# Two layers on a graph of 3327 nodes on one core: products with v spread one, none, two over three rounds, side pieces in other rounds, counts of adj in a row of their own

## The chip, the core and the metric

The kernel runs on one core of one Trainium2 chip. The metric is the device time of one execution in microseconds (us); the time before is the median of three executions. All views come from one profiled execution of the program.

Engines are named as in the profile: PE multiplies matrices (PEld is its loading of weights), ACT applies functions such as the exponential, DVE and POOL work element by element, SP issues nearly all DMAs. Each engine has its own queue, and the engines wait for each other through semaphores.

## The reference, cut to what matters

N = 3327 nodes with 128 features, adj a 0/1 matrix of N x N with about 0.24% ones and a full diagonal.

```python
# layer 0
H = X @ W.T + b;  s = H @ a_s;  r = H @ a_r
e = leaky_relu(A * s + A * r.T, 0.2)
att = softmax(where(A > 0, e, NEG), axis=1)
x = layernorm(x + att @ H)
# layer 1, n = 3327, d = 128, h = 8
q = (x @ Wq.T).reshape(d, n, h)      # k and v likewise
a = einsum('dnh,dmh->dnm', q, k) * d ** -0.5
a = softmax(a + adj + adj, axis=2)
out = einsum('dnm,dmh->dnh', a, v).reshape(n, h * d) @ Wo.T
x = layernorm(x + out)
```

Because of the reshape, layer 1 has 128 independent attentions ("d") of 3327 queries and 3327 keys, each with only 8 numbers per key. Their 128 x 3327 x 3327 exponentials are nearly the whole work. adj is added twice; the kernel takes the exponential with a scale of 2, so it adds adj once to half-scaled scores, or multiplies the exponential by a factor made of adj (e squared where adj is 1, else 1).

## The kernel before, in words

**Main work.** The 128 attentions go in 32 groups of four; each group has seven blocks of 476 queries (the last 472), so there are 224 blocks. In a block the 26 tiles of 128 keys are taken in 26 rounds. Two plans alternate: even blocks take eight threes of key tiles and then a pair (24, 25); odd blocks take tile 25, then eight threes, then tile 24. A round works on two halves of tiles; a half is two of the four attentions, 128 x 952 numbers.

A three is a *stretch* of three rounds, here called A, B, C. Its first tile, x, is handled on ACT and POOL: scores on PE (L152), an exponential straight from the scores (L1172), and a multiplication by the factor on POOL (L1173). The other two are added on DVE: scores plus adj (L1175), and in a later round one exponential over both halves, 128 x 1904 (L991).

| round | scores and what follows |
|---|---|
| A | half 1 of x; half 0 of the first added tile |
| B | half 0 of x; half 1 of the first added tile |
| C | both halves of the second added tile |

Score banks: one for x, two for added tiles, so x's scores in B wait until ACT has read those of A. Round 1 of an even block issues its two pairs of scores in reverse order.

**Products with v** (L956, `products`): one key tile against v for four attentions, eight matmuls summed into a single bank `av` over the block. `multiply` puts the round's tile into the list `waiting` and multiplies the tile four rounds back (LAG = 4), so each round has one product, behind the round's scores and side piece on PE. The tile is one that ACT or POOL finished in earlier rounds. After a block's last product DVE copies `av` out (L966), and the next block's first product waits for that copy. In odd blocks the copy is put between the two adds of round 3 (`between`).

**Side pieces.** Layer 0 for the later row tiles, the projections to q, k and v, and the results of layer 1 are cut in pieces and slipped into the rounds. Two rows hold them in order. `main` has, for each of 25 row tiles, 26 products (26 key tiles with weighed adj, L241), the normalization and twelve projections, and later the results; `aside` has the weighing and masking of adj on POOL (L308, L317; nine pieces of each for a row tile, three key tiles a piece) and the counts of adj on DVE (L326; 18 pieces) and, in between, the loads of adj. Kinds are p (PE), d (DVE), l (DVE, a round later), m (POOL), x (issues DMAs); `n` entries wait for a mark and `t` entries set one. `lane` says in which rounds one piece of a kind may go: before, p, d and m in the rounds for which `reading` holds (round 1 of every three, counted from the first three, with exceptions at the ends of a block), so in B of a stretch.

`aside` is a strict order: weighing and masking of one chunk of adj (six pieces), then the six counts of a chunk, then the load of a later chunk.

**The first seven blocks** also make the factors of adj on POOL (L793), stretch by stretch, and store them; later blocks load them.

The nested functions that the diff touches stand in the order-building part of the kernel; nothing in it is chosen at run time, so each engine's order is fixed when the program is built.

Of the kernel before, what the change touches and what calls it, by code (L numbers as in the profile page):

```python
# [17 lines left out]
P = 128  # L18
# [29 lines left out]
def kernel(  # L48
# [29 lines left out]
    H = wqT.shape[1]  # L78
# [71 lines left out]
    def special():  # L150
# [9 lines left out]
        with ExitStack() as sx, tc.manual_schedule(engines=ALL):  # L160
# [9 lines left out]
            CH = [(i, min(i + CW, NT)) for i in range(0, NT, CW)]  # L170
# [96 lines left out]
            def layer0(t, side=True, trow=None, bank=bank, held=None):  # L267
# [5 lines left out]
                s = {"a": {}, "w": {}}  # L273
                q0 = t * len(CH)
# [55 lines left out]
                def product(i):  # L330
                    if i == 0:
                        s["p"] = bank()
                    (by_columns if side else whole)(
                        s["p"][:, : D + 1],
                        s["w"][i // CW][: kr[i], i % CW, :],
                        hsb[: kr[i], i, :],
                        r,
                        start=(i == 0),
                        stop=(i == NT - 1),
                    )  # L340
# [124 lines left out]
                for n, (i0, i1) in enumerate(CH):  # L465

                    aside.append(("n", ("P", q0 + n - 2, 0)))
                    for c0 in range(i0, i1, 3):
                        c1 = min(c0 + 3, i1)
                        aside.append(("m", lambda n=n, c0=c0, c1=c1: weigh(n, c0, c1)))  # L470
                        aside.append(("m", lambda n=n, c0=c0, c1=c1: mask(n, c0, c1)))
                    aside.append(("t", ("W", q0 + n)))
                    c = [("d", lambda n=n, h=h, k=k: count(n, h, k)) for h in range(3) for k in range(2)]
                    counts.append(c)
                    main.append(("n", ("W", q0 + n, 3)))
                    if i1 == NT:
                        main.append(("m", biased))
                    main += [("p", lambda i=i: product(i)) for i in range(i0, i1)] + [("t", ("P", q0 + n))]
                    aside.append(counts[-1])
                return loads, main + chain + [("t", ("rows", t))], aside  # L480

            def result(t):
# [116 lines left out]
                units += [("p", lambda: turn(0, 2, 0)), ("p", lambda: turn(2, 4, 2))]  # L599
                units += [("d", lambda: divided(0, 2, 0)), ("d", lambda: divided(2, 4, 2))]  # L600
                units += [("p", lambda: turn(4, 5, 0)), ("d", lambda: divided(4, 5, 0))]
                units += [("p", lambda h=h: project(h)) for h in range(H)]
                root = rsqrt(s, lambda: s["st"][:r, 7:8], r)
                units += [("d", finish), ("d", together(variance, *root[:3]))]
                return units + [("d", together(*root[c : c + 3])) for c in (3, 6, 9)] + [("d", scale)]
# [368 lines left out]

            waiting = []

            def multiply(s, i):
                waiting.append((s, i))
                while len(waiting) > LAG:
                    products(*waiting.pop(0))  # L980

# [20 lines left out]

            def reading(n, odd):

                n -= odd
                if n % 3 == 1 and 4 <= n < NR - 2:  # L1010
                    return True
                return n in ((NR - 2,) if odd else (0, NR - 1))

            def lane(kind, n, odd):

                if kind == "l":
                    return int(reading(n - 1, odd) if n else True)
                return int(reading(n, odd) or kind == "p" and n - odd == 3)

            made = [layer0(t) for t in range(1, NT)]  # L1020
            first_loads = made[0][0]
            main = []
            aside = []
            for n, (_, m, a) in enumerate(made):

                later = []
                for u in a:
                    if u[0] == "r":

                        at = max((k for k, v in enumerate(aside) if v[0] == "n"), default=0)  # L1030
                        aside.insert(at, ("x", u[1]))
                    elif isinstance(u, list):
                        ahead = made[n + 1][0][sum(isinstance(v, list) for v in later)] if n + 1 < len(made) else None
                        later.append(u)
                        if n:
                            aside += u + [ahead] * (ahead is not None)
                    else:
                        aside.append(u)
                if n == 0:

                    for k, u in enumerate(later):
                        aside += u + [made[1][0][k]] * (len(made) > 1)
                main.append(m)
            main.append([("n", ("counts", 0, 0))] + judge())
            aside.append(("t", ("counts", 0)))
            results = [((needs[t] + 1) * total + LAG + 6, result(t)) for t in range(NT - 1)]
            end = result(NT - 1)
            marks = {("P", q): 0 for q in range(len(CH))}
            side = {"main": [], "aside": aside, "since": {"main": 0, "aside": 0}, "read": -2}

            def head(row, now, force=False):

                while True:
                    if not side[row]:
                        if row == "aside":
                            return None
                        ahead = ("rows", reads[min(max(now, 0) // total + 2, NG - 1)]) in marks
                        if results and results[0][0] <= now and (ahead or not main):
                            side[row] = results.pop(0)[1]
                        elif main:  # L1060
                            side[row] = main.pop(0)
                        else:
                            return None
                    kind, f = side[row][0]
                    if kind == "t":
                        marks[f] = now
                    elif kind == "w":
                        if not force and now - side["since"][row] < f:
                            return None
                    elif kind == "n":  # L1070
                        if f[:2] not in marks or not force and now - marks[f[:2]] < f[2]:
                            return None
                    else:
                        return kind
                    side[row].pop(0)
# [4 lines left out]

            def work_tensor(now, n, odd):

                for _ in range(lane("p", n, odd) if side["read"] != now - 1 else 0):
                    if head("main", now) != "p":
                        break
                    run("main", now)

            def work(now, n, odd):
                room, low, pool = lane("d", n, odd), lane("l", n, odd), lane("m", n, odd)
                for row in ("main", "aside"):  # L1090
                    while True:
                        kind = head(row, now)
                        if kind == "x":
                            pass
                        elif kind == "d" and room:
                            room -= 1
                            if row == "main":
                                side["read"] = now
                        elif kind == "l" and low:
                            low -= 1  # L1100
                            side["read"] = now
                        elif kind == "m" and pool:
                            pool -= 1
                        else:
                            break
                        run(row, now)

            def finish_to(mark, now):
                while mark not in marks:
                    row = "main" if head("main", -1 if now is None else now, True) else "aside"  # L1110
                    if head(row, -1 if now is None else now, True) is None:
                        break
                    run(row, -1)
                    tick(True)
# [13 lines left out]
            for g in range(NG):  # L1128
                k4, v4, _ = group
                for b in range(NBLK):  # L1130
# [5 lines left out]
                    for n, rnd in enumerate(rounds):  # L1136
# [16 lines left out]
                        for j in range(HG):  # L1153
                            if n == NR // 2 + j * (NR > 12) and (b + 1 < NBLK or g + 1 < NG):
                                queries[1](j)
                        sc = {}
                        for i, h, z in reversed(rnd) if n == 1 and not odd else rnd:
                            sc[i, h] = (pe if z is None else pd).tile([P, 2, 512], F32, name="scb")
                            for t in range(2):
                                pair_scores(sc[i, h][: kr[i], t, :w], s.k4, s.q4, i, kr[i], 2 * h + t, w)  # L1160
                        work_tensor(g * total + at, n, odd)
                        between = odd and n == LAG - 1
                        for (i, h, at_) in rnd:
                            if between and h == 1:
                                multiply(s, order[n])
                            r, z = kr[i], sc[i, h]
                            if i not in s.e:
                                s.e[i] = sp.tile([P, HG, WB], F32, name="e4")
# [13 lines left out]
                        if n + 1 in starts or n + 1 == NR:  # L1182
                            del adjs[m]
                            make_factor(m + 1)
                        if not between:
                            multiply(s, order[n])
                        work(g * total + at, n, odd)
            exp_late(NG * total + 2)
            finish_to(None, NG * total + LAG + 6)
# [384 lines left out]
```

## Time and profile before

| what | value |
|---|---|
| time, median of 3 | 10050.16 us (10049.41 to 10050.97) |
| profiled execution, its own time | 10052.42 us |
| its span, first to last instruction | 10050.6 us |
| mean granted PE clock | 0.995 |
| exponentials from scores, L1172 | 3920, mean 1000 ns |
| late exponentials, L991 | 3920, mean 1810 ns |
| POOL's multiplies, L1173 | 3920, mean 2236 ns |
| DVE's adds, L1175 | 7728, mean 1142 ns |
| products, L956 | 46592 matmuls (8 a tile), mean 573 ns |

How to read it: spans of instructions that follow each other on ACT or POOL overlap a little, so the mean of one is longer than the distance from its start to the next one's start. Matmuls of four row or column parts run side by side, so PE's time for a product is the distance from its start to the start of what follows. Busy shares are means over the whole span; where an engine is late is seen in the timeline.

### The profile page before, as it was taken

What the parts mean: (1) busy time and instruction counts of PE and PEld (TensorE: products, weight loads), DVE (VectorE), ACT (ScalarE), POOL (GpSimd) and SP (SyncE); (2) the same over time, 40 slices, a digit from 0 to 9 for tenths busy, and PEclk for the clock granted to TensorE, in tenths of its full rate; (3) what the DMA queues carried; (4) which work ended last, traced back from release to release, by engine and by line L of the source; (5) the groups of instructions that cost most, each with busy time, mean ns of one, the idle gap of its engine ahead of it and who ended that gap; (6) DMA issues with size and microseconds to landing.
All of it is one profiled execution on the core that took longest, in us unless ns stands there. A gap on an engine that the chain in (4) does not pass through costs nothing.

```text
span 10050.6 us, 207550 instructions
## 1 busy us (share of the span) xinstructions
PE 9477.4 (94%) x79523; PEld 3013.9 (30%) x79523; DVE 9188.5 (91%) x10554; ACT 9897.6 (98%) x7904; POOL 9177.2 (91%) x4954
## 2 busy tenths in 40 slices
PE   7999999999999999999999999999999999999998
PEld 2233333333233233323333333333333233222222
DVE  7899999999999999999999999999999999888888
ACT  7999999999999999999999999999999999999998
POOL 7999999999999999999999999999999999888887
PEclk9999999999999999999999999999999999999999
DMA  6765656665665656565566656566665565555554
GB/s 194 209 179 179 179 168 183 178 176 168 181 173 171 183 167 189 168 184 170 169 179 187 176 172 179 176 170 178 181 179 175 171 175 168 169 158 166 164 164 132
DMA packets 1399414, 1755.28 MB, mean 175 GB/s; under 512 B 349360, under 2 KB 1386890, under 8 KB 1394312
## 3 DMA queue, kind: packets, MB, share of 16 engines
q1 hardware_dynamic: 1388061, 1739.30, 59.7%
q8 instruction: 626, 10.26, 0.4%
q10 hardware_dynamic: 10347, 2.61, 0.1%
q14 instruction: 380, 3.11, 0.1%
HBM read 1637.49 MB, written 103.93 MB: 173 GB/s over the span
## 4 chain that ended last, share of the span: by engine, by line
ACT 41%; PE 21%; POOL 16%; issue 13%; DVE 7%; DMA 2%; SPq 1%; POOLq 0%; ACTq 0%; DVEq 0%
ACT e L991 29%; POOL e L1173 15%; ACT e L1172 11%; PE av L956 11%; PE scb L152 9%; DVE e L1175 5%; PE bank L241 1%; DVE o L966 1%; DMA q4b<-qT 1%; DMA at<-in_adjT_dram 1%; POOL w L308 0%; SPq L733 0%; POOL w L317 0%; DMA k4b<-kT 0%; POOL at L793 0%
## 5 line engine op out<-in xcount | busy, mean ns | idle before, releaser
L1173 POOL TENSOR_TENSOR e<-e,at 128x952 f32<-128x952 f32 (+1 forms) x3920 | 8715.9, 2236 | 788.6 <-ACT e L1172 735.1
L1175 DVE TENSOR_TENSOR e<-scb,at 128x952 f32<-128x952 f32 (+1 forms) x7728 | 8499.4, 1142 | 769.7 <-PE scb L152 650.1
L991 ACT ACTIVATE e<-e 128x1904 f32<-128x1904 f32 (+3 forms) x3920 | 7095.9, 1810 | 26.4 <-DVE e L1175 11.1
L956 PE MATMUL av<-e,v4b 128*32 128x476 f32 (+1 forms) x46592 | 5843.8, 573 | 99.0 <-DVE o L966 68.0
L152 PE MATMUL scb<-q4b,k4b 32*128 32x476 f32 (+1 forms) x23296 | 3882.4, 486 | 440.8 <-ACT e L1172 361.9
L1172 ACT ACTIVATE e<-scb 128x952 f32<-128x952 f32 (+1 forms) x3920 | 3921.1, 1000 | 74.9 <-PE scb L152 36.7
L152 PEld LDWEIGHTS scb<-q4b,k4b 32*128 32x128 f32 (+1 forms) x23296 | 1779.3, 189 | 5459.2 <-ACT e L1172 3161.5
L956 PEld LDWEIGHTS av<-e,v4b 128*32 128x32 f32 (+1 forms) x46592 | 1014.1, 109 | 1239.9 <-issue 933.4
L241 PE MATMUL bank<-hsb,w 128*32 128x129 f32 (+1 forms) x5200 | 278.6, 286 | 0.0
L326 DVE TENSOR_SCALAR_CACHE_REDUCE dump<-a 128x384 bf16<-128x384 f32 (+2 forms) x468 | 247.3, 528 | 0.6
L308 POOL TENSOR_SCALAR w<-trow,er 128x129 f32<-128x129 f32 x650 | 231.6, 376 | 1.3
L317 POOL TENSOR_TENSOR w<-w,a 128x384 f32<-128x384 f32 (+3 forms) x225 | 207.9, 924 | 0.1
L966 DVE COPY o<-av 128x476 f32<-128x476 f32 (+1 forms) x224 | 145.2, 648 | 31.3 <-PE av L956 30.4
L241 PEld LDWEIGHTS bank<-hsb,w 128*32 128x32 f32 (+1 forms) x5200 | 102.9, 108 | 148.2 <-issue 148.2
L241 PE MATMUL bank<-wo,ot 128*32 128x128 f32 x1600 | 85.2, 285 | 0.0
L402 DVE TENSOR_SCALAR hi<-bank 128x256 fp32r<-128x256 f32 (+1 forms) x200 | 83.0, 415 | 0.0
L409 DVE SCALAR_TENSOR_TENSOR lo<-bank,hi 128x256 fp32r<-128x256 f32 (+1 forms) x200 | 83.0, 415 | 0.0
L241 PE MATMUL bank<-wk,x1T 128*32 128x256 f32 x800 | 63.9, 391 | 0.0
L241 PE MATMUL bank<-wq,x1T 128*32 128x256 f32 x800 | 63.9, 391 | 0.0
L241 PE MATMUL bank<-wv,x1T 128*32 128x256 f32 x800 | 63.9, 391 | 0.0
L502 PE MATMUL bank<-ident,o 128*128 128x128 f32 x225 | 52.0, 304 | 0.0
L290 POOL MEMSET a<- 128x128 f32 (+1 forms) x25 | 5.2, 208 | 44.4 <-DVE dump L326 44.4
(123 smaller groups left out, 647.3 us busy)
## 6 DMA issues: line engine op xcount, KB each, us to landing
at<-in_adjT_dram SPq DMA_DIRECT2D x1536, 476.0 KB
at<-ftd SPq DMA_DIRECT2D x1674, 238.0 KB
at<-in_adjT_dram SPq DMA_DIRECT2D x256, 472.0 KB
at<-ftd SPq DMA_DIRECT2D x279, 236.0 KB
k4b<-kT SPq DMA_DIRECT2D x128, 415.9 KB
q4b<-qT SPq DMA_DIRECT2D x1528, 29.8 KB
at<-in_adjT_dram SPq DMA_DIRECT2D x192, 208.2 KB
at<-in_adjT_dram SPq DMA_DIRECT2D x150, 238.0 KB
```

What stands on the lines that cost most here:

```text
L152: nc.tensor.matmul(dst, k4[32 * j : 32 * j + H4, first_key(i) : first_key(i) + 2 * r - 1 : 2], q4[32 * j : 32 * j + H4, :nb], start=True, ...
L241: nc.tensor.matmul(dst[c0:c1], w[:, c0:c1], mov, **kw)
L308: nc.gpsimd.tensor_scalar(w, s["t"][:, :, :T3], -LOWEST, e, op0=ALU.min, op1=ALU.max)
L317: nc.gpsimd.tensor_tensor(w, w, s["a"][n][:, c0 - i0 : c1 - i0, :r], op=ALU.mult)
L326: nc.vector.tensor_scalar(z, a, float(k), None, op0=ALU.is_equal, op1=ALU.add, accum_out=even[:, t, at : at + 1])
L402: nc.vector.tensor_scalar(hi[:r, o : o + QW], s["b"][:r, :QW], scale, None, op0=ALU.mult)
L956: nc.tensor.matmul(s.av[32 * j : 32 * j + 32, : s.w], s.v4[:r, j, i * H1 : i * H1 + 32], e[:r, j, : s.w], start=(s.left == NT - 1), stop=( ...
L966: nc.vector.tensor_copy(o4[:, :w], s.av[:, :w])
L991: nc.scalar.activation(e, e, AF.Exp, scale=2.0)
L1172: nc.scalar.activation(eh, z[:r, :, :w], AF.Exp, scale=2.0)
L1173: nc.gpsimd.tensor_tensor(eh, eh, ah, op=ALU.mult)
L1175: nc.vector.tensor_tensor(eh, z[:r, :, :w], ah, op=ALU.add)
```

## The change

The products: B (`place` 1) has none, A (`place` 0) one, and C (`place` 2) two, the first of them between its two pairs of scores. `between` goes, so in odd blocks the copy of `av` comes behind both adds. The side pieces: one p, d or q in A, q also in B, m in B, l in C (q is the new name for the layer-0 products and the results' projections, so these may come twice in a stretch). The counts leave `aside` for a third row, `counts`, together with the loads of adj that follow them; marks L tell `aside` that a chunk's load has been issued, and the loads wait with marks W until the chunk before has been weighed and masked. The numbers of all pieces are as before.

```diff
-                        between = odd and n == LAG - 1
-                        for (i, h, at_) in rnd:
-                            if between and h == 1:
-                                multiply(s, order[n])
+                        for i, h, at_ in rnd:
...
+                        place = (n - odd) % 3
                         for i, h, z in reversed(rnd) if n == 1 and not odd else rnd:
+                            if place == 2 and h == 1:
+                                multiply(1)
                             sc[i, h] = (pe if z is None else pd).tile([P, 2, 512], F32, name="scb")
...
-                        if not between:
-                            multiply(s, order[n])
+                        waiting.append((s, order[n]))
+                        multiply(int(place != 1))
...
-            def multiply(s, i):
-                waiting.append((s, i))
-                while len(waiting) > LAG:
-                    products(*waiting.pop(0))
+            def multiply(k):
+                for _ in range(k):
+                    if len(waiting) > LAG:
+                        products(*waiting.pop(0))
...
-            def reading(n, odd):
+            def lane(kind, n, odd):
                 n -= odd
-                if n % 3 == 1 and 4 <= n < NR - 2:
-                    return True
-                return n in ((NR - 2,) if odd else (0, NR - 1))
-
-            def lane(kind, n, odd):
                 if kind == "l":
-                    return int(reading(n - 1, odd) if n else True)
-                return int(reading(n, odd) or kind == "p" and n - odd == 3)
+                    return int(n % 3 == 2)
+                if kind == "q" and n % 3 == 1:
+                    return 1
+                if kind == "m":
+                    return int(n % 3 == 1)
+                if n % 3 != 0:
+                    return 0
+                return int(kind in "pq" or n > 3 or n == 0 and odd)
...
+                    aside.append(("n", ("L", q0 + n, 0)))
...
-                    main += [("p", lambda i=i: product(i)) for i in range(i0, i1)] + [("t", ("P", q0 + n))]
+                    main += [("q", lambda i=i: product(i)) for i in range(i0, i1)] + [("t", ("P", q0 + n))]
...
-                units += [("p", lambda h=h: project(h)) for h in range(H)]
+                units += [("q", lambda h=h: project(h)) for h in range(H)]
...
                     elif isinstance(u, list):
-                        ahead = made[n + 1][0][sum(isinstance(v, list) for v in later)] if n + 1 < len(made) else None
-                        later.append(u)
-                        if n:
-                            aside += u + [ahead] * (ahead is not None)
+                        counts += u
+                        if n + 1 < len(made):
+                            counts += [("n", ("W", (n + 1) * len(CH) + k, 0)), made[n + 1][0][k], ("t", ("L", (n + 2) * len(CH) + k))]
+                        k += 1
...
-                for _ in range(lane("p", n, odd) if side["read"] != now - 1 else 0):
-                    if head("main", now) != "p":
-                        break
+                kind = head("main", now)
+                if kind in ("p", "q") and lane(kind, n, odd) and side["read"] != now - 1:
                     run("main", now)
...
-                for row in ("main", "aside"):
+                for row in ("main", "aside", "counts"):
```

More of the change, by code (lines that the diff above doesn't have):

```diff
@@ L1022, in special @@
             main = []
-            aside = []
+            aside, counts = [], []
             for n, (_, m, a) in enumerate(made):
-                later = []
+                k = 0
                 for u in a:
                     if u[0] == "r":
-                        at = max((k for k, v in enumerate(aside) if v[0] == "n"), default=0)
+                        at = max((k for k, v in enumerate(aside) if v[0] == "n" and v[1][0] == "P"), default=0)
                         aside.insert(at, ("x", u[1]))
                     elif isinstance(u, list):
-                        ahead = made[n + 1][0][sum(isinstance(v, list) for v in later)] if n + 1 < len(made) else None
-                        later.append(u)
-                        if n:
-                            aside += u + [ahead] * (ahead is not None)
+                        counts += u
+                        if n + 1 < len(made):
+                            counts += [("n", ("W", (n + 1) * len(CH) + k, 0)), made[n + 1][0][k], ("t", ("L", (n + 2) * len(CH) + k))]
+                        k += 1
                     else:
                         aside.append(u)
-                if n == 0:
-                    for k, u in enumerate(later):
-                        aside += u + [made[1][0][k]] * (len(made) > 1)
                 main.append(m)
             main.append([("n", ("counts", 0, 0))] + judge())
-            aside.append(("t", ("counts", 0)))
+            counts.append(("t", ("counts", 0)))
             results = [((needs[t] + 1) * total + LAG + 6, result(t)) for t in range(NT - 1)]
@@ L1048, in special @@
             marks = {("P", q): 0 for q in range(len(CH))}
-            side = {"main": [], "aside": aside, "since": {"main": 0, "aside": 0}, "read": -2}
+            marks.update({("L", len(CH) + k): 0 for k in range(len(CH))})
+            side = {"main": [], "aside": aside, "counts": counts, "since": {}, "read": -2}
             def head(row, now, force=False):
@@ L1054, in head @@
                     if not side[row]:
-                        if row == "aside":
+                        if row != "main":
                             return None
@@ L1109, in finish_to @@
                 while mark not in marks:
-                    row = "main" if head("main", -1 if now is None else now, True) else "aside"
-                    if head(row, -1 if now is None else now, True) is None:
+                    at = -1 if now is None else now
+                    row = next((row for row in ("main", "aside", "counts") if head(row, at, True)), None)
+                    if row is None:
                         break
```

## The prediction

> **What bounds the kernel now.** I read the page's busy line first, then the timeline of a calm stretch, then the starts of blocks, then the list of waits. A stretch is three rounds A, B, C over three key tiles: x (exponential from scores, then multiplied on POOL; two halves, x1 in A, x0 in B) and two added tiles (added on DVE, exponential late in one piece).
>
> ```profile
> PE 9477.4 (94%) x79523; PEld 3013.9 (30%) x79523; DVE 9188.5 (91%) x10554; ACT 9897.6 (98%) x7904; POOL 9177.2 (91%) x4954
> ```
>
> ACT leads at 98%, but the other three have only 6 to 9% to spare, so what matters is where one of them makes ACT late. A calm stretch, from the timeline (start, us, engine, line):
>
> ```profile
> 4519.93 2.23 POOL L1173 TENSOR_TENSOR e<-e,at 128x952 f32<-128x952 f32 x1 [0.25 <-ACT e L1172]
> 4521.38 1.00 ACT L1172 ACTIVATE e<-scb 128x952 f32<-128x952 f32 x1
> 4522.22 1.84 ACT L991 ACTIVATE e<-e 128x1904 f32<-128x1904 f32 x1
> 4522.51 2.23 POOL L1173 TENSOR_TENSOR e<-e,at 128x952 f32<-128x952 f32 x1 [0.35 <-ACT e L1172]
> 4523.90 1.01 ACT L1172 ACTIVATE e<-scb 128x952 f32<-128x952 f32 x1
> 4524.63 1.00 PE L956 MATMUL av<-e,v4b 128*32 128x476 f32 x8
> 4524.75 1.84 ACT L991 ACTIVATE e<-e 128x1904 f32<-128x1904 f32 x1
> 4526.43 1.01 ACT L1172 ACTIVATE e<-scb 128x952 f32<-128x952 f32 x1
> ```
>
> ACT starts an exponential of scores 0.84 us before its next instruction and a late one 1.68 us before: 5.05 us a stretch, nothing between. Spans overlap by 0.16 us, so lateness has to be read from starts, not from idle time. POOL has two multiplies of 2.19 us (back to back) and two gaps, 0.25 and 0.35. The multiply that ends at 4522.16 completes a tile that PE takes at 4524.63: 2.47 us of room.
>
> The start of an even block, same view:
>
> ```profile
> 4971.66 1.06 ACT L1172 ACTIVATE e<-scb 128x952 f32<-128x952 f32 x1
> 4972.77 0.49 PE L152 MATMUL scb<-q4b,k4b 32*128 32x476 f32 x2 [0.28 <-ACT e L1172]
> 4973.19 1.00 PE L956 MATMUL av<-e,v4b 128*32 128x476 f32 x8
> 4974.13 0.50 PE L152 MATMUL scb<-q4b,k4b 32*128 32x476 f32 x4
> 4974.23 1.91 ACT L991 ACTIVATE e<-e 128x1904 f32<-128x1904 f32 x1
> 4974.56 1.01 PE L956 MATMUL av<-e,v4b 128*32 128x476 f32 x8
> 4975.49 0.93 PE L152 MATMUL scb<-q4b,k4b 32*128 32x476 f32 x4
> 4976.08 0.96 ACT L1172 ACTIVATE e<-scb 128x952 f32<-128x952 f32 x1
> 4976.97 1.80 ACT L991 ACTIVATE e<-e 128x1904 f32<-128x1904 f32 x1
> 4977.91 0.64 DVE L966 COPY o<-av 128x476 f32<-128x476 f32 x1
> 4978.61 1.01 PE L956 MATMUL av<-e,v4b 128*32 128x476 f32 x8 [0.24 <-DVE o L966]
> 4978.67 0.94 ACT L1172 ACTIVATE e<-scb 128x952 f32<-128x952 f32 x1
> 4979.70 1.79 ACT L991 ACTIVATE e<-e 128x1904 f32<-128x1904 f32 x1
> 4981.63 0.97 ACT L1172 ACTIVATE e<-scb 128x952 f32<-128x952 f32 x1
> ```
>
> Distances between ACT's starts: 4974.23 to 4976.08 is 1.85 (0.17 over 1.68), 4978.67 to 4979.70 is 1.03 (0.19 over 0.84), 4979.70 to 4981.63 is 1.93 (0.25 over). The first is PE's: here three score exponentials come in three rounds, and PE, which needs the end of x1 at 4972.72 for the next x's score bank, can't bring round 3's scores in time. The other two follow the copy: PE stands still until the single product bank is read, then DVE and PE run late. Over all blocks after 500 us these three places sum to 0.27 + 0.17 + 0.24, say 0.67 us an even block; an odd block loses 0.33 us at one place (its copy sits between two adds). 1.0 us a pair of blocks, 112 pairs: 112 us. The waits agree that the copy is met in every block:
>
> ```profile
> PEld av L956 <- DVE o L966: 127.9, 222, 1.1
> ```
>
> [...] at 4978.61 all of PE waits for the copy, and a piece on POOL stands ahead of the next multiply. [...] two pairs of scores together take 0.42 us from start to next start (4974.13 to 4974.56), one pair alone 0.42 as well (4972.77 to 4973.19), a product 0.93 (4974.56 to 4975.49). I go by these rows.
>
> **The change part by part.** The work is the same; only its order moves.
>
> *Products.* B loses its product; C has scores of one half, product, scores of the other half, product. C's pairs no longer overlap: 0.42 us of PE more per stretch. What has to fit: from the end of x1 (1.03 us after its start) to the next x1, PE has 5.05 - 1.03 - 0.05 (semaphore) - 0.57 (scores to ACT) = 3.40 us. Before: 0.42 + 0.93 + 0.42 + 0.93 = 2.70, and 0.25 for a side piece in B. After: 0.42 + 0.42 + 0.93 + 0.42 + 0.93 = 3.12, or 3.37 with a side piece of the new kind q in B. It fits inside ACT's time, by 0.28 and by 0.03; cost 0 there.
>
> *Even blocks.* Round 3's lateness was 0.27; its chain gains 0.42 and loses the 0.06 by which DVE held up scores: 0.63. With a q in round 1, which the built order has in 19 of the 112 even blocks, 0.25 more. The new block's first product comes in C of the second stretch, a round later than now, so the copy (ready about 0.6 us after A's add) holds up nobody: the other two places go. 112 x 0.63 + 19 x 0.25 = 75 us.
>
> *Odd blocks.* The copy now stands behind both adds of C, so the late exponential is in time. But the next product comes at once, in A: three adds end at 0.57 + 3 x 1.06 = 3.75 after x1's end, the copy at 4.40, the product runs 4.46 to 5.39, and B's scores start 0.33 late. The chain's 0.28 takes most of it: 0.05 to 0.08 is left, and 0.25 more where B has a q (38 of 112). 112 x 0.08 + 38 x 0.25 = 18 us. Block starts: 75 + 18 - 112 = -19 us.
>
> *POOL's pieces.* Counts leave the row that holds weighing and masking. Before, six pieces in six stretches are followed by six counts, in which POOL recovers: the longest runs after the first seven blocks are 7 pieces. After, only the load of the next chunk stops them: the built order has 22 runs of 19 stretches in a row, one for each row tile. A weighing piece takes 1.02 us up to the next multiply (4981.90 to 4982.92), a masking one 0.92 (4987.41 to 4988.33); with the shorter ones of the last chunks and the bias, 0.91 on average. POOL's spare time is 87.5 (ACT, two blocks) - 35 x 2.19 = 10.8 us in 17 stretches, 0.64 each. So a run adds 0.27 us of lag each stretch. In the block around 4370 us, with six pieces, the room before the product shrinks from 2.46 to 1.15, 0.22 each: it agrees. The room is 2.47, and 0.2 of PE's chain behind it: 2.67. A run of 7 costs nothing; one of 19 makes 5.2, less 2.67, less 0.8 that ACT loses at the two block starts inside it anyway: 1.7 us. 22 x 1.7 = 37 us. What is late: POOL's multiply, then the x product on PE, then the scores behind it, then x1 on ACT.
>
> *The first seven blocks.* There POOL also makes the factors (0.67 us a stretch, back to back): 4.38 + 0.67 = 5.05, no spare time at all, so each piece costs its 0.91. The built order has 33 pieces there, against 25: 8 x 0.91 = 7 us.
>
> *Counts, main's d pieces, DMAs.* Counts and other DVE pieces move from B to A, where DVE waits 0.57 us or more for B's scores (0.63 by the chain above), and the usual piece takes 0.42 to 0.62: cost 0; two bigger ones a row may cost 0.2 us, 25 rows: up to 5. Loads of adj chunks go to SP at least 38 rounds (64 us) ahead of the mask, as before never close; SP may wait for the buffer for some us, under a lookahead of three stretches (15 us). Products of adj's weights are asked for at least 5 rounds behind the last mask but twice, so PE doesn't wait. Main's 39 products and projections a row take fewer stretches, which ACT never sees.
>
> Sum: -19 + 37 + 7 = +25 us. The profiled execution took 10052.4 (span 10050.6 and 1.8 around it), so 10077 for it; the median of the three runs is 10050.2, so 10075.
>
> **Rivals.**
> 1. *POOL's lag is hidden.* If a run grows by 0.14 or less a stretch, or the room is 5 us, the 22 runs cost nothing, and -19 + 7 and what partial stalls add gives about 10040 to 10050. For it: no stall of ACT on POOL is to be seen now after 500 us. Against: the measured shrinking, 0.22 to 0.27.
> 2. *Faster: the copy was all of the block starts.* If round 3's scores are late only as an echo of the copy and of side pieces, even blocks lose nothing and odd ones 0.08: 112 - 9 = 103 gained; POOL's runs then have no relief, 22 x 2.5 = 55, and 7: -41, 10009. It decides at round 3 of an even block: its exponential within 1.7 us of the one before. Against: at 4976.08 it is late before the copy of 4977.91 has begun.
> 3. *PE becomes the bound.* The chain with q has 0.03 us to spare. [...] 399 stretches with q in B lose up to 0.07 to 0.1 each and the even blocks 0.1: +40 to 50 on the forecast, about 10120. The point is 3.40 us from x1 to x1.
>
> That the change doesn't do what it says is no case: the built order shows it.
>
> **How the numbers follow.** Forecast 0.52, rival 1 0.25, rival 2 0.10, rival 3 0.13. The forecast's own range, 10057 to 10092, comes from product pitches of 0.91 to 0.94 and rooms of 2.4 to 3. To keep eight in ten, the range runs from 10030 (rival 1 inside, rival 2 outside) to 10110 (the lower part of rival 3 inside). About 0.2%, 20 us, is what can be told from no change: faster than 10030 is rival 2 and an edge of rival 1, 0.11; slower than 10070 is the larger part of the forecast (0.42), rival 3 and a little of rival 1, 0.58; between them 0.31.
>
> **What would show it.** Right: ACT's starts after round 3 of even blocks late by 0.6 and none by the copy; PE's wait for DVE's copy (127.9 us on PEld) much smaller; PE waiting for POOL's multiply at the end of each run of 19 (tens of us in all, now 0.4 on PE after 500 us); the first 375 us some 7 longer. Wrong: no wait for POOL (rival 1), round 3 in time (rival 2), ACT late in ordinary q stretches (rival 3).

## The result and the profile after

| what | before | after |
|---|---|---|
| time, median of 7 runs | 10049.56 us (10049.02 to 10050.97) | 10085.74 us (10077.35 to 10092.33) |
| ratio to before, 95% interval | | 1.0036 [1.0024, 1.0047] |
| profiled execution, span | 10052.42, 10050.6 us | 10089.09, 10087.3 us |
| mean granted PE clock | 0.995 | 0.994 |

The change costs 36 us, against 25 forecast. Line numbers shift: products are L957, the copy of `av` L967, the late exponential L992, x's exponential L1170, POOL's multiply L1171, DVE's add L1173. The page's busy line of after:

```profile
PE 9223.2 (91%) x79523; PEld 2697.4 (27%) x79523; DVE 9173.1 (91%) x10554; ACT 9898.8 (98%) x7904; POOL 9188.4 (91%) x4954
```

The same instructions, and ACT's busy time has grown by 1.2 us of 36: the loss lies between its instructions. The list of waits between 500 and 9000 us (us in all, times, longest):

```profile
PEld av L957 <- DVE o L967: 97.1, 176, 1.1
ACT e L1170 <- PE scb L152: 51.3, 145, 2.8
PE av L957 <- POOL e L1171: 46.5, 120, 0.9
PE av L957 <- DVE o L967: 30.1, 63, 0.8
```

The same list of the kernel before, in which PE's wait for POOL's multiply is 0.4 us (once):

```profile
PEld av L956 <- DVE o L966: 106.5, 192, 1.1
PE av L956 <- DVE o L966: 55.1, 112, 0.8
ACT e L1172 <- PE scb L152: 7.5, 8, 1.5
```

So PE now waits for POOL, and ACT for PE. The copy is still met: PEld's wait for it fell only from 106.5 to 97.1 us in this window (the forecast's 127.9 is that of the whole run, where it is 117.5 now), which is not "much smaller". The start of an even block shows what that means. The timeline, ACT's and the chain's rows:

```profile
4995.07 0.31 PEld L152 LDWEIGHTS scb<-q4b,k4b 32*128 32x128 f32 x4 [0.30 <-ACT e L1170]
...
4995.70 1.06 ACT L1170 ACTIVATE e<-scb 128x952 f32<-128x952 f32 x1
...
4995.72 1.00 PE L957 MATMUL av<-e,v4b 128*32 128x476 f32 x8
4996.54 1.90 ACT L992 ACTIVATE e<-e 128x1904 f32<-128x1904 f32 x1
4996.65 0.49 PE L152 MATMUL scb<-q4b,k4b 32*128 32x476 f32 x2
...
4997.07 1.01 PE L957 MATMUL av<-e,v4b 128*32 128x476 f32 x8
4998.01 0.50 PE L152 MATMUL scb<-q4b,k4b 32*128 32x476 f32 x4
...
4998.60 0.96 ACT L1170 ACTIVATE e<-scb 128x952 f32<-128x952 f32 x1 [0.16 <-PE scb L152]
4999.46 1.78 ACT L992 ACTIVATE e<-e 128x1904 f32<-128x1904 f32 x1
...
4999.71 0.64 DVE L967 COPY o<-av 128x476 f32<-128x476 f32 x1
5000.40 0.16 PEld L957 LDWEIGHTS av<-e,v4b 128*32 128x32 f32 x8 [0.37 <-DVE o L967]
...
5001.15 0.96 ACT L1170 ACTIVATE e<-scb 128x952 f32<-128x952 f32 x1
...
5001.99 1.79 ACT L992 ACTIVATE e<-e 128x1904 f32<-128x1904 f32 x1
```

Round 3's exponential starts 2.06 us after the late one before it (4996.54 to 4998.60), 0.38 over 1.68. After the copy ACT's starts are 1.69 and 0.84 apart: the first product waits for the copy, and nobody waits for that product.

The new wait, from the timeline inside a run of POOL pieces:

```profile
4845.59 4.41 POOL L1171 TENSOR_TENSOR e<-e,at 128x952 f32<-128x952 f32 x2
...
4849.98 1.07 POOL L308 TENSOR_SCALAR w<-trow,er 128x129 f32<-128x129 f32 x3
...
4850.05 1.01 PE L957 MATMUL av<-e,v4b 128*32 128x476 f32 x8 [0.29 <-POOL e L1171]
...
4851.00 4.42 POOL L1171 TENSOR_TENSOR e<-e,at 128x952 f32<-128x952 f32 x2
...
4854.96 1.79 ACT L992 ACTIVATE e<-e 128x1904 f32<-128x1904 f32 x1
4855.38 0.96 POOL L317 TENSOR_TENSOR w<-w,a 128x384 f32<-128x384 f32 x1
...
4855.48 1.01 PE L957 MATMUL av<-e,v4b 128*32 128x476 f32 x8 [0.36 <-POOL e L1171]
4856.31 4.40 POOL L1171 TENSOR_TENSOR e<-e,at 128x952 f32<-128x952 f32 x2
4856.42 0.49 PE L152 MATMUL scb<-q4b,k4b 32*128 32x476 f32 x4
4857.01 0.96 ACT L1170 ACTIVATE e<-scb 128x952 f32<-128x952 f32 x1 [0.25 <-PE scb L152]
```

POOL has no gap left: its pairs of multiplies start 5.41 and 5.31 us apart (4845.59, 4851.00, 4856.31), against ACT's 5.05. The multiply ends at 4855.42, the product starts at 4855.48, the scores behind it at 4856.42, and x1 on ACT comes 2.05 us after 4854.96, 0.37 late. That is the chain that the prediction named.

**Where the time is.** To place all of it I took, in each trace, the distance between neighbouring starts on ACT and subtracted the calm distance of that instruction (0.843 us for scores of 128x952, 1.682 for a late one of 128x1904, 0.888 for a late one of 128x952, 1% less in the narrower seventh blocks). What is left is lateness. Block starts are the places that the prediction names: in even blocks from x1 of round 3 to x1 of round 6, in odd ones from the late exponential of round 4 to x1 of round 7. The half-clock row takes, behind the first seven blocks, the lateness from 2 us before to 6 us after a time in which PE's granted clock was 0.5. Both kernels were profiled twice (the second profiles are from the last experiment):

| lateness of ACT, us | before | before again | after | after again |
|---|---|---|---|---|
| first seven blocks | 32.7 | 32.4 | 41.1 | 40.7 |
| block starts, over 60 ns each | 97.0 | 97.8 | 72.2 | 71.2 |
| other places, over 60 ns each | 8.6 | 7.7 | 36.5 | 36.0 |
| under 60 ns each | 9.8 | 9.7 | 24.1 | 20.8 |
| beside times of PE at half clock | 12.6 | 11.5 | 23.2 | 25.6 |
| span | 10050.6 | 10046.9 | 10087.3 | 10083.5 |

The first pair: +8 in the first seven blocks, -25 at block starts, +28 in other places, +14 small delays, +11 at half clock; together +36, with 1 us more in the tail and half a microsecond less ahead of the first row. The two profiles of each kernel agree row by row within about 3 us.

### The profile page after: what moved, and what is told of

Read it like the earlier page. It is cut to its first block, busy times and chain, and to the rows that moved or that the text cites. A ratio compares the mean times of both kernels' runs of the same rounds, so it can differ in the third digit from the quotient of the medians.

```text
span 10087.3 us, 207506 instructions
## 1 busy us (share of the span) xinstructions
PE 9223.2 (91%) x79523; PEld 2697.4 (27%) x79523; DVE 9173.1 (91%) x10554; ACT 9898.8 (98%) x7904; POOL 9188.4 (91%) x4954
## 4 chain that ended last, share of the span: by engine, by line
PE 42%; DVE 18%; ACT 14%; POOL 13%; issue 7%; DMA 4%; SPq 1%; DVEq 0%; ACTq 0%; POOLq 0%
PE scb L152 20%; PE av L957 20%; DVE e L1173 16%; POOL e L1171 11%; ACT e L1170 10%; ACT e L992 4%; DMA at<-in_adjT_dram 2%; PE bank L241 2%; POOL w L308 1%; POOL w L317 1%; DMA q4b<-qT 1%; DVE o L967 1%; DVE dump L326 1%; DVE lo L409 0%; DMA v4b<-vd 0%
## 5 line engine op out<-in xcount | busy, mean ns | idle before, releaser
L1171 POOL TENSOR_TENSOR e<-e,at 128x952 f32<-128x952 f32 (+1 forms) x3920 | 8732.0, 2242 | 811.7 <-ACT e L1170 746.9
L1173 DVE TENSOR_TENSOR e<-scb,at 128x952 f32<-128x952 f32 (+1 forms) x7728 | 8461.3, 1143 | 843.9 <-PE scb L152 595.6
L992 ACT ACTIVATE e<-e 128x1904 f32<-128x1904 f32 (+3 forms) x3920 | 7066.7, 1803 | 5.1 <-DVE e L1173 5.1
L957 PE MATMUL av<-e,v4b 128*32 128x476 f32 (+1 forms) x46592 | 5859.8, 575 | 129.1 <-POOL e L1171 76.7
L152 PE MATMUL scb<-q4b,k4b 32*128 32x476 f32 (+1 forms) x23296 | 3494.6, 473 | 701.3 <-ACT e L1170 461.9
L1170 ACT ACTIVATE e<-scb 128x952 f32<-128x952 f32 (+1 forms) x3920 | 3893.3, 993 | 130.9 <-PE scb L152 95.1
L152 PEld LDWEIGHTS scb<-q4b,k4b 32*128 32x128 f32 (+1 forms) x23296 | 1489.4, 190 | 5580.8 <-ACT e L1170 3029.8
L957 PEld LDWEIGHTS av<-e,v4b 128*32 128x32 f32 (+1 forms) x46592 | 981.5, 108 | 1471.5 <-issue 1091.0
L967 DVE COPY o<-av 128x476 f32<-128x476 f32 (+1 forms) x224 | 144.4, 644 | 8.9 <-PE av L957 8.3
```

Source lines behind the costliest of these rows:

```text
L152: nc.tensor.matmul(dst, k4[32 * j : 32 * j + H4, first_key(i) : first_key(i) + 2 * r - 1 : 2], q4[32 * j : 32 * j + H4, :nb], start=True, ...
L957: nc.tensor.matmul(s.av[32 * j : 32 * j + 32, : s.w], s.v4[:r, j, i * H1 : i * H1 + 32], e[:r, j, : s.w], start=(s.left == NT - 1), stop=( ...
L967: nc.vector.tensor_copy(o4[:, :w], s.av[:, :w])
L992: nc.scalar.activation(e, e, AF.Exp, scale=2.0)
L1170: nc.scalar.activation(eh, z[:r, :, :w], AF.Exp, scale=2.0)
L1171: nc.gpsimd.tensor_tensor(eh, eh, ah, op=ALU.mult)
```

## The experiments

Theory: the change gains at block starts and loses in the runs of POOL pieces, the two parts separable. Rivals: PE's longer chain is what costs, everywhere; or POOL's wait merely takes the place of another.

**The products alone**, on the kernel before: none in B, two in C, `between` gone; rows and side pieces as before.

```diff
-            def multiply(s, i):
-                waiting.append((s, i))
-                while len(waiting) > LAG:
-                    products(*waiting.pop(0))
+            def multiply(k):
+                for _ in range(k):
+                    if len(waiting) > LAG:
+                        products(*waiting.pop(0))
...
+                            if place == 2 and h == 1:
+                                multiply(1)
...
+                        waiting.append((s, order[n]))
+                        multiply(int(place != 1))
```

> The kernel before with the new places of the products alone; side pieces and counts stay where they were. Theory (three terms: block starts shorter by about 20 us, lag of POOL in runs of pieces about 37, the first seven blocks about 7): no runs on POOL here, so -20 for the block starts; but side pieces now stand in B in most stretches, where the chain from x1 to x1 has 3.12 + 0.25 = 3.37 us of 3.40, and a projection of 0.5 makes it 3.6, late by 0.2 in some 300 stretches: +60. About +40, 10090, with ACT late in ordinary stretches and no new wait for POOL. Rival (the products alone are what makes the changed kernel slower, at block starts): +36 with all of it at block starts. Rival (the products alone are a gain): 10030.

Measured: 10116.94 us (10113.35 to 10117.34), ratio 1.0065 [1.0048, 1.0081]. The waits between 500 and 9000 us:

```profile
ACT e L1172 <- PE scb L152: 33.7, 137, 2.4
...
PE av L956 <- POOL e L1173: 0.9, 2, 0.7
```

Block starts fall by 44 us to 53.2, ordinary places rise from 8.6 to 76.9 and the small delays from 9.8 to 45.5; PE waits for POOL 0.9 us in all. So the late places are x1's in ordinary stretches, PE's chain and not POOL, as expected; the size was missed, 66 us where about 40 was expected. The product placement by itself loses.

**The side pieces and the rows alone**: the changed kernel with one product a round and `between` again.

```diff
-            def multiply(k):
-                for _ in range(k):
-                    if len(waiting) > LAG:
-                        products(*waiting.pop(0))
+            def multiply(s, i):
+                waiting.append((s, i))
+                while len(waiting) > LAG:
+                    products(*waiting.pop(0))
...
+                            if between and h == 1:
+                                multiply(s, order[n])
```

> The changed kernel with the products put back to one a round (and the copy of odd blocks between the adds); new places of side pieces and the counts row stay. Theory: the block starts are those of before (112 us), POOL's runs and the first blocks stay (+44): at least 10094. Side pieces of DVE in A now come where DVE has no gap with this order of products (its gap lies between the adds of B and C), so each pushes B's add by 0.3 us in some of 1200 stretches: up to +80 more, 10100 to 10180. Rival (side pieces and counts are harmless, the products did it): 10050.

Measured: 10146.36 us (10145.8 to 10148.06), ratio 1.0094 [1.0077, 1.011]. The waits:

```profile
PE scb L152 <- DVE e L1173: 109.6, 311, 1.6
PE av L957 <- DVE o L967: 78.5, 125, 1.2
PE av L957 <- POOL e L1171: 35.2, 95, 0.6
```

The first was 22.3 us before and is 22.5 in the changed kernel. PE now waits for DVE's adds, so side pieces in A need the products out of B. Each part alone loses more than the two together (+66 us for the products, +95 for the rest, +36 together).

**The counts' own row alone**, on the kernel before.

```diff
-                        ahead = made[n + 1][0][sum(isinstance(v, list) for v in later)] if n + 1 < len(made) else None
...
+                        counts += u
+                        if n + 1 < len(made):
+                            counts += [("n", ("W", (n + 1) * len(CH) + k, 0)), made[n + 1][0][k], ("t", ("L", (n + 2) * len(CH) + k))]
...
-                for row in ("main", "aside"):
+                for row in ("main", "aside", "counts"):
```

> The kernel before with the counts and the loads of adj in a row of their own, alone; products and side pieces stay. Theory: POOL's runs come with this part: about +25 to +40, 10075 to 10090, PE's wait for POOL's multiply some tens of us after 500 us; block starts as before. Rival (the counts row is harmless): 10050.

Measured: 10078.77 us (10076.04 to 10084.97), ratio 1.0028 [1.0017, 1.0039], as expected. The wait:

```profile
PE av L957 <- POOL e L1172: 22.5, 47, 1.0
```

The products are placed as before here, so this wait comes of the row alone. First seven blocks 44.9 (before 32.7), block starts 103.6 (97.0), other places 19.1 (8.6).

**POOL's pieces in every second stretch**, on the changed kernel. First over the whole run:

```diff
                 if kind == "m":
-                    return int(n % 3 == 1)
+                    return int(n % 6 == 1)
```

> The changed kernel with the weighing and masking pieces in every second stretch only. Theory: a piece of 0.91 us in every second stretch is under POOL's 0.64 of spare time a stretch, so the lag never grows: POOL's runs cost nothing after the first seven blocks, -37 against the changed kernel, about 10045 to 10050, and PE's wait for POOL's multiply near 0 after 500 us. Rival (PE's chain with two side pieces is the loss): no change, 10085. Rival (block starts are the loss): no change.

Measured: 10066.29 us (10061.57 to 10072.18, 20 runs), ratio 1.0016 [1.0009, 1.0022], short of what was expected. POOL's runs cost nothing any more (other places 11.6, and no wait of PE for POOL is left in the list), but the edit spoiled the first group: what comes behind POOL's pieces was not done when the next group needed it, and 22 pieces, projections on PE and the handling of their results on DVE, came in one burst (first seven blocks 55.5 us, 41.1 in the changed kernel). Busy time of the engines in that stretch (length; PE, PEld, DVE, ACT, POOL with the number of instructions; granted clock, DMA share, GB/s):

```profile
385.00:395.00 10.00, 7.28 (x48) 1.60 (x44) 3.69 (x7) 0.00 (x0) 0.59 (x1) 0.50 0.39 120
```

ACT does nothing in these 10 us. So once more, with the thinning only behind the first group:

```diff
+                if now >= total and (n - odd) // 3 % 2:
+                    pool = 0
```

> The changed kernel, with a piece of aside's weighing or masking on POOL only in every second stretch from the second group on (the first seven blocks stay as they are). The earlier run with every second stretch throughout took POOL's waits away but let the first group run out of time, so that 22 pieces came in one burst near 385 us. Theory (POOL's runs of 19 pieces cost what it loses outside block starts): 28 us of the changed kernel's losses go, the first group is as there, so 30 to 40 us under it, 10045 to 10055; PE's wait for POOL's multiply after 500 us falls from 46.5 to under 3 us. Rival (PE's longer chain is what costs, and POOL's wait only stands in its place): the wait goes, the time stays within 10 us of 10086.

Measured: 10051.99 us (10047.63 to 10058.01, 13 runs), ratio 1.0005 [0.9997, 1.0013]: the median is 34 us under that of the changed kernel, inside what was expected. Other places fall from 36.5 to 10.4, block starts hardly move (67.5), small delays stay (22.7). The wait of ACT is left, PE's for POOL is not:

```profile
PE av L957 <- DVE o L967: 47.8, 74, 0.8
ACT e L1172 <- PE scb L152: 33.2, 96, 2.6
```

POOL's lag was a cost of its own and stood in place of nothing.

**No q in B in the first two stretches of a block**, on top:

```diff
                 if kind == "q" and n % 3 == 1:
-                    return 1
+                    return int(n > 6)
```

> As the kernel before it in this list (POOL's pieces in every second stretch), and a piece of the kind q goes into B only from the third stretch of a block on. Theory: a q in B of the first two stretches lengthens PE's chain where it has least room (0.25 us in 19 even and 38 odd blocks, 14 us), so 8 to 14 us less than that kernel, some 10040. Rival (the chain absorbs a q there as elsewhere, 3.37 of 3.40 us): within 3 us of it.

Measured: 10030.02 us (10023.29 to 10038.06, 20 runs), ratio 0.9982 [0.9975, 0.9989]: 22 us under the last one, more than the 8 to 14 expected. In the two profiles block starts fall by 17.0 us (67.5 to 50.5), the lateness beside half-clock times by 7.2 (17.3 to 10.1).

**Round 0 of even blocks without a side piece on PE and with two products**, on top of that:

```diff
-                return int(kind in "pq" or n > 3 or n == 0 and odd)
+                return int(kind in "pq" and (n > 0 or odd) or n > 3 or n == 0 and odd)
...
+                        if n == 0 and not odd:
+                            multiply(1, LAG - 1)
```

> As the kernel before it in this list, and in round 0 of an even block PE has no side piece and issues two products in place of one, so that round 2 has one product less. Theory (the lateness of round 3 in even blocks comes from the products between the end of x1 in round 1 and the scores of round 3): that chain is shorter by 0.93 us, the lateness falls from 0.56 to 0.2 us or less in 112 blocks: 15 to 35 us less, 10010 to 10025, under the kernel before the change. Rival 1 (the lateness is set by the x score bank alone): no gain, within 5 us. Rival 2 (two products in round 0 make x's scores late there in turn): the lateness moves to rounds 1 or 2, within 10 us.

Measured: 10019.91 us (10015.22 to 10021.62), ratio 0.9971 [0.9959, 0.9982]: 28 us under the kernel before, the fastest here. It is 10 us under the last one, where 15 to 35 was expected. The timeline at the start of an even block:

```profile
4957.22 1.80 PE L957 MATMUL av<-e,v4b 128*32 128x476 f32 x16
...
4959.74 1.06 ACT L1172 ACTIVATE e<-scb 128x952 f32<-128x952 f32 x1
4960.69 0.49 PE L152 MATMUL scb<-q4b,k4b 32*128 32x476 f32 x2 [0.86 <-DVE e L1175]
4960.73 1.79 ACT L992 ACTIVATE e<-e 128x1904 f32<-128x1904 f32 x1
...
4962.65 0.96 ACT L1172 ACTIVATE e<-scb 128x952 f32<-128x952 f32 x1
```

Round 3 is 0.24 late here (4960.73 to 4962.65, 1.92), 0.24 on average against 0.35 with the products as in the changed kernel. But PE now waits 0.86 for DVE's adds ahead of round 2's scores (that group of waits grew from 12.1 to 97.1 us), and the late exponential of 4960.73 starts 0.15 late: 11 us in 83 even blocks that were not there. That is as much as round 3 gained (37.5 to 26.0 us in all), so rival 2 is right on where the lateness went. The theory fails: from the end of x1 to round 3's scores PE takes 2.96 us (median), against 2.98 in the kernel before it in this list, for the wait stands where the product was. Why the time fell by 10 us all the same is open: the two profiled executions lie 5.8 us apart, with 2 us of it at x1 of round 7 in odd blocks.

**Both kernels again**, unchanged, for a second profile.

> The changed kernel itself, once more, for a second profile. In the first, 36 us of ACT's lateness stand beside stretches of 3.4 or 6.8 us in which PE's granted clock was 0.5 (12 of them), against 23 us (10) in the kernel before. Theory (these dips come by chance, and their number differs between executions): the span less the time lost at dips is again 10051, within 5 us, however many dips this profile has. Rival (the changed order brings the dips on): 12 or more dips and 35 us or more again.

> The kernel before itself, for a second profile. Theory (dips by chance): the span less the time lost at dips is again 10027, within 5 us; the number of dips may well differ from 10. Rival (fewer dips belong to its order): 10 dips or fewer and about 23 us again.

Measured: 10082.12 us (10080.76 to 10085.35), ratio 1.0032 [1.002, 1.0045], and 10047.58 us (10043.47 to 10050.48), ratio 1.0 [0.9991, 1.0008]. The theory of chance missed: over the whole run the half-clock times of the changed kernel now hold 45 us (14 of them), and 10083.5 less that is 10038, not 10051; in the kernel before they hold 27 (11), and 10046.9 less that is 10020, not 10027. Part of the miss was my sorting: in the first seven blocks lateness beside half clock and lateness from POOL can't be told apart, and counted together there, as in the table, the rows repeat. Behind them the rival is nearer: 23.2 and 25.6 us after, 12.6 and 11.5 before.

## Why the prediction was right, and where not

Time, range and sign held: 10075 forecast, 10085.7 measured. By its own steps (lateness beside half clock left out):

- **Even blocks, 75 us: place right, sizes wrong twice.** Round 3 lost 0.18 us a block before and 0.45 after (46 us in 103 blocks); 0.27 and 0.63 were forecast. The 0.27 had the lateness beside half clock in it (28.2 us in 107 blocks). "Its chain gains 0.42" is the mis-sized term: from the end of x1 to the start of round 3's scores PE takes 2.77 us before and 2.98 after (medians without a q), 0.21 more. The reverse order of round 1 puts x's pair of scores right ahead of C's first pair, and from the first to the product behind them it is 0.64 us (4995.07 to 4995.72 above is 0.65), not two times 0.42: a pair behind a pair adds 0.22. So with the products alone moved round 3 lost 0.31, with everything moved and no q in round 1 0.35 (84 blocks). A q in round 1 cost more than its 0.25: 0.89 in the 19 blocks with one, so 0.54 more. It parts the two pairs, and the chain grows to 3.53: by 0.55, of which 0.36 is the piece itself (see below) and about 0.2 the pair that now stands alone. The two errors nearly cancel in the forecast for blocks with a q.
- **The copy: right in effect.** No lateness follows it in even blocks; that it would hold up nobody was wrong (PEld waits 97.1 us for it).
- **Odd blocks, 18 us: close.** 23 us; 0.15 us without a q in B (0.05 to 0.08 forecast), 0.34 with one (37 blocks; 0.33 forecast).
- **Block starts, -19: measured -25.**
- **Runs of 19 POOL pieces, +37: the mechanism right, the size a third smaller.** Other places rose by 28 us, and 26 of these went with the thinned pieces: 1.3 us for each of 22 runs in place of 1.7.
- **First seven blocks, +7: measured +8.**
- **"It fits inside ACT's time, by 0.28 and by 0.03; cost 0 there": wrong by 14 us.** The margin of 0.03 rests on 0.25 for a q, read where a product follows it. From the first matmul of such a piece to the next group's first is 0.245 us in the trace of before (the median of 1112, ahead of a product); ahead of scores, where the change puts it in B, 0.357 (the median of 381). So the chain is 3.48 of 3.40 us; the trace has 3.50 (median), from the start of x's scores in B to that of the next x1's. This is where rival 3 put its loss. Its 0.1 was an assumption; the piece measured 0.11 longer (0.357 less 0.245), and the price is a third of rival 3's: of the small delays 8.9 us stand at x1 exponentials with a side piece of PE in the 3.4 us ahead of them, where there were none before, and 7.7 at the late exponentials right behind an x1, with such a piece ahead, against 2.4. From the third stretch of a block on the two cases can be compared: the next x1 is 0.043 us late in the median of 203 stretches with a q in B and not at all in that of 880 without; its scores start 3.55 and 3.19 us after the end of the x1 before. With POOL's pieces thinned it is the same, 0.042 us in 232 stretches, so POOL is not the cause. Why the piece takes longer ahead of scores is not shown.
- **Half clock, +11: not in the forecast.**

The rivals: 1 fell (PE waits 46.5 us for POOL; with that lag taken away the time is 10052); 2 fell at the point that the prediction named (round 3 is late ahead of the copy); 3 is true in small. -25 + 28 + 8 + 14 + 11 is +36; the three terms that the forecast had priced came to +11, 14 less than its +25, and the two that it had at nothing added 25. That the total came out closer than its parts is luck.

The prediction took the parts as terms of a sum. They are not: the side pieces' new rounds need the products out of B and the other way round. With POOL's pieces thinned the two together are level with the kernel before (1.0005), and with the q's out of the first two stretches they gain (0.9982).

## What to carry to other kernels

Give a helper engine's side pieces by their mean spacing, not by their order alone: a longer run of pieces at an unchanged total cost next to nothing here (runs of up to 7 before: 0.4 us of PE's wait between 500 and 9000 us) until the lag, piece by piece, had used the room ahead of its consumer (2.47 us); from there on it turned into lateness (1.3 us a run of 19, for 1.7 forecast). Cost a moved piece by what will stand behind it on its engine, not by what stood behind it before: 0.245 became 0.357 us, and the 0.42 of a pair of scores became 0.22 behind another pair. Where an engine at 98% is fed by three at 91 to 94%, read the lateness from start-to-start distances and sort it by place; the busy shares say nothing of it.

## What the hardware showed beside that

Between 420 and 9980 us PE's granted clock falls to 0.5 for 3.4 or 6.8 us at a time, six times in the trace of before and six in that of after, in kernels whose PE is busy for 94 and 91% of the span. One such place in the changed kernel, in windows of 3.4 us (columns as above):

```profile
2946.40:2949.80 3.40, 2.40 (x20) 0.96 (x18) 2.86 (x6) 3.40 (x4) 2.81 (x3) 1.00 0.58 156
2949.80:2953.20 3.40, 3.40 (x18) 0.79 (x20) 1.78 (x3) 3.15 (x3) 3.40 (x2) 0.50 0.85 274
2953.20:2956.60 3.40, 3.40 (x20) 0.49 (x12) 2.01 (x2) 1.05 (x2) 0.80 (x2) 0.50 0.00 0
2956.60:2960.00 3.40, 3.20 (x28) 0.82 (x24) 3.07 (x5) 3.40 (x3) 3.09 (x2) 0.99 0.10 20
```

PE is busy 2.40 of 3.40 us (0.71), then at half clock for two windows in which it has no gap, and ACT does 1.05 us of work in the second. In the changed kernel's trace all such times between 420 and 9980 us begin on one grid of 3.413 us, to within 0.001 of a window. The profile's busy time tells only in part which windows are hit: the windows just ahead of the six times in the changed kernel were busy to 0.55 to 0.73 (median of all windows 0.94), those of the kernel before to 0.72 to 0.82 (median 0.96). Few of the less busy windows are followed by one: in the changed kernel 25 of 2801 lie under 0.75, and six of these 25 are.

How the order enters is open, but the place is not: of the half-clock times between 420 and 9980 us, two profiles of each kernel, 10 of 11 before and 11 of 13 after begin in round 1 or 2 of an even block. Windows under 0.75 are 25 and 21 in the two profiles after and 7 in both before, and after 11 of the 13 half-clock times last 6.8 us, before none of 11; but the fastest kernel has 46 such windows and only two such times. The grid begins 1.50 us behind the first instruction in the trace of before and 0.71 us behind it in that of after, and other blocks are hit (from 2223.6, 2578.6 and 7275.3 us on before, from 2949.8, 7305.2 and 8534.0 after). That such shifts are why single runs of the changed kernel lie 15 us apart and of the kernel before 2 us in the same comparison is my guess, which no run here tested.
